# A transformer block's last additions: seven of eight moved beside the expert blocks, and cut in halves

## The chip, the cores and the metric

The kernel runs on one core of one Trainium2 chip. The metric is device microseconds of one execution. Before the change three runs took 1761.9, 1764.81 and 1767.08 us, median 1764.81 us. A separate execution was taken by the hardware profiler; all durations below come from that one.

## The reference, cut to what matters

`x` holds 8 batches of 512 tokens of 256 numbers, all float32. Four layers follow each other, each added to `x` after a layer norm: a decaying scan with projections, a mixture of experts, causal attention with 16 heads, and the same mixture of experts again.

```python
x = L0_attn_a_x                                  # (8, 512, 256)
x = x + scan(_layernorm(x), ...)
x = x + ffn(_layernorm(x), ...)                  # mixture 0
x = x + attention(_layernorm(x), ...)
x = x + ffn(_layernorm(x), ...)                  # mixture 1: the last thing computed
```

In a mixture a router picks 4 of 16 experts for every token (groups of four experts first, then the best in the two best groups), with weights that add up to 2.5. The output is the weighted sum of the four experts' outputs, plus that of shared experts that take every token:

```python
topk_idx, tw = _route(x, router_w, bias)
routed = sum over the 4 chosen e of tw[e] * ((silu(x @ gate_w[e]) * (x @ up_w[e])) @ down_w[e])
return routed + shared(x)
```

`setup_inputs(seed=0)` draws the inputs, so the number of tokens that each expert gets is fixed by the seed.

## The kernel before, in words

**Four stages.** Scan, mixture 0, attention, mixture 1. While a layer goes batch by batch, the router and the shared experts of the mixture behind it run beside it, and each token's row is scattered to DRAM (`xg`), into the regions of its four experts. When all batches are through, `routed(i, table, beside)` (L802) works off the experts' rows in blocks of 128.

**The blocks and their order.** Every expert's region is cut into blocks of 128 rows; within a region the tokens of batch 0 lie first, then those of batch 1, and so on. `blocks` writes the table of blocks: first the first block of every expert, then the second of every expert that has one, and so on. The program is built for `LIKELY` = 136 blocks (table entries behind the last real block do no harm); only if there are more does a branch run the other seven first.

**One block.** `load(n)` on SP's queue brings 128 rows from `xg` (L838). `fetch(n)` copies the expert's gate and up weights (ACT and DVE, L846). `turn(n)` transposes the rows on PE, `up(n)` does the gate and up products on PE (L864), sigmoid on ACT (L872) and two products on DVE (L873, L874), and the row's weight for this expert (L877, L885). `down(n)` does the last product (L892), ACT scales it by that weight (L900), and an indirect DMA on POOL's queue adds the 128 rows to the result in DRAM (L901). The result stands in two halves, `parts[1][0]` and `parts[1][1]`: even blocks add to the one, odd blocks to the other. The first also holds the layer's input, the second the shared experts' output. A scatter to a part waits until the one before it on the same part has landed.

**The loop.** `run` (L911) issues, for block n: the load of n + 2, the fetch of n + 1, `up(n)`, `turn(n + 1)`, `down(n - 2)`. Rows live in nine buffers (tag `kb4`), and a buffer is free again when the scatter of its block has landed. Behind `down(k - 1)` the loop calls what stands under key k in `beside`:

```python
if n - 2 >= first:
    down(n - 2)
    for work_beside in beside.get(n - 1, ()):
        work_beside()
```

**The last additions.** A batch's output is the sum of the two parts' rows of that batch. `sum_of(b, ...)` (L1387) loads both, 512 KB each, 4 KB for each of 128 partitions; `add_up` (L1398) adds them in one DVE instruction of 128 x 1024 (L1399) and stores 512 KB (L1402). `SUMMED` (L62) says for five batches after how many blocks this may be done beside the blocks, with all its DMAs on POOL's queue, where the scatters are too:

```python
SUMMED = {0: DONE[0], 1: 76, 2: 88, 3: 110, 4: 127}     # DONE[0] = 64
```

The loads go in at that key, the addition and the store eight blocks later. Batches 5, 6 and 7 are summed at the end (`at_the_end`, L1452), with part 0 loaded on SP's queue and part 1 on ACT's.

**The check.** Whether a batch is really complete after that many blocks depends on the routing. `check(b)` (L1420) works it out on DVE, at block 10 + 4b: `upto[b]` holds each expert's count after batch b; `most` is the largest of these counts in blocks, rounded up; `done` is the sum over all experts of min(the expert's blocks, `most`); the batch counts as late if `done > SUMMED[b]`. `checked` (block 40) adds up the late ones into `late`. Batch 0 is not checked, since after 64 blocks it is complete in any case. Behind the blocks SP, ACT and DVE load `late` (L1455) and branch (L1462): if it is above zero, all batches in `SUMMED` are summed once more at the end, and then those that are not in it:

```python
with tc.If(again > 0):
    for b in SUMMED:
        at_the_end(b)
for b in range(B):
    if b not in SUMMED:
        at_the_end(b)
```

**Order.** A scheduling layer sets the final order on each engine from the order written; what is marked `keep_in_program_order` stays where it is written. Every engine and every queue works in order. On POOL's queue a load of a sum waits for the last scatter to its part, and the next scatter to that part waits until the load has landed.

Of the kernel before, what the change touches and what calls it, by code (L numbers as in the profile page):

```python
# [10 lines left out]
FP = mybir.dt.float32  # L11
# [4 lines left out]
P = 128  # L16
B, T, D = 8, 512, 256
NT = T // P
# [22 lines left out]
LIKELY = TK * NTOK // BLK + E // 2  # L41
# [6 lines left out]
DONE = [min(E * (b + 1) * NT, NBLK) for b in range(B)]  # L48
# [6 lines left out]
KB, COLS = 9, 6  # L55
# [3 lines left out]
HELD = 6  # L59


SUMMED = {0: DONE[0], 1: 76, 2: 88, 3: 110, 4: 127}  # L62
PICKS = 5
ES, QK = 6, 6
ATT_SCALE = 0.25
# [9 lines left out]
def tile_hybrid_block(  # L75
# [22 lines left out]
    nc = tc.nc  # L98
# [3 lines left out]
    work = ctx.enter_context(tc.tile_pool(name="work", bufs=2))  # L102
# [8 lines left out]
    def banks_of(**many):  # L111
        pools = ExitStack()
        for kind, bufs in many.items():
            stage[kind] = pools.enter_context(
                tc.tile_pool(name=f"ps_{kind}", bufs=bufs, space=bass.MemoryType.PSUM)
            )
        return pools
# [7 lines left out]
    parts = [[dram.tile([NTOK + BLK, D], FP, name=f"part_{i}_{j}") for j in range(2)] for i in range(2)]  # L125
# [3 lines left out]
    def values(name: str):  # L129
        return work.tile([P, NT * (H * VC + 32 - VC)], FP, tag="v", name=name)  # L130
# [82 lines left out]
    def load_expert(e: int):  # L213
# [13 lines left out]
        out=before,  # L227
        in_=before,
# [20 lines left out]
    def load_attention_weights():  # L249
# [16 lines left out]
        out=causal, in_=causal, compare_op=ALU.is_ge, fill=0.0, base=0, pattern=[[0, 2], [1, P]], channel_multiplier=-1  # L266
# [6 lines left out]
        out=tri, in_=tri, compare_op=ALU.is_gt, fill=0.0, base=0, pattern=[[1, P]], channel_multiplier=-1  # L273
# [324 lines left out]
    def choices(i: int, b: int, tag: str, held, paced: bool):  # L598
# [59 lines left out]
        counts[i] = row[:, NT, :]  # L658
        if i == 1 and b in SUMMED:
            upto[b] = small.tile([1, E], FP, tag=f"upto_{b}", name=f"upto_{b}", bufs=1)  # L660
# [722 lines left out]
    with banks_of(big=4, misc=2, y=2):  # L1383

        beside = (nc.gpsimd, nc.gpsimd)

        def sum_of(b: int, homes, queues=(nc.sync, nc.scalar)):  # L1387

            both = []
            for j, queue in enumerate(queues):  # L1390
                both.append(homes(j))
                queue.dma_start(  # L1392
                    out=both[j],
                    in_=parts[1][j][b * T : (b + 1) * T, :].rearrange("(p t) d -> p (t d)", p=P),
                )
            return both

        def add_up(b: int, both, queues=(nc.sync, nc.scalar)):  # L1398
            added = nc.vector.tensor_add(both[0], both[0], both[1])  # L1399
            if queues is beside:  # L1400
                tc.keep_in_program_order(added)
            queues[b % 2].dma_start(out=out[b].rearrange("(p t) d -> p (t d)", p=P), in_=both[0])  # L1402

        sums = {}

        def early(b: int):
            def homes(j: int):
                tile = xpool.tile([P, NT, D], FP, tag="x", name=f"sum_{b}_0") if j == 0 else values(f"sum_{b}_1")
                return tile.rearrange("p t d -> p (t d)") if j == 0 else tile[:, 0 : NT * D]

            return {
                SUMMED[b]: [lambda: sums.update({b: sum_of(b, homes, beside)})],
                SUMMED[b] + 8: [lambda: add_up(b, sums.pop(b), beside)],
            }

        late = small.tile([1, 1], I32, tag="late", name="late", bufs=1)
        lates = small.tile([1, len(SUMMED)], FP, tag="lates", name="lates", bufs=1)
        nc.gpsimd.memset(lates, 0.0)

        def check(b: int):  # L1420


            nb = table[4]
            one = small.tile([1, E + 2], FP, tag="one", name=f"one_{b}", bufs=1)
            n, most, done = one[:, 0:E], one[:, E : E + 1], one[:, E + 1 : E + 2]
            nc.vector.tensor_sub(n, upto[b], region[0:1, :])
            shape = [1, E, NJ]
            more = work.tile(shape, FP, tag="col", name=f"above_{b}", bufs=COLS)
            nc.vector.tensor_tensor(
                more, n.unsqueeze(2).to_broadcast(shape), steps[0:1, :].unsqueeze(1).to_broadcast(shape), ALU.is_gt  # L1430
            )
            nc.vector.tensor_reduce(n, more, AX.X, ALU.add)
            nc.vector.tensor_reduce(most, n, AX.X, ALU.max)
            nc.vector.tensor_scalar(n, nb[0:1, :], most, None, ALU.min)
            nc.vector.tensor_reduce(done, n, AX.X, ALU.add)
            nc.vector.tensor_scalar(lates[:, b : b + 1], done, float(SUMMED[b]), None, ALU.is_gt)

        def checked():
            any_late = small.tile([1, 1], FP, tag="any_late", name="any_late", bufs=1)
            nc.vector.tensor_reduce(any_late, lates, AX.X, ALU.add)  # L1440
            nc.vector.tensor_copy(late, any_late)

        plan = {}
        for b in SUMMED:
            for at, do in early(b).items():
                plan.setdefault(at, []).extend(do)
            if SUMMED[b] < DONE[b]:
                plan.setdefault(10 + 4 * b, []).append(lambda b=b: check(b))
        plan.setdefault(40, []).append(checked)
        routed(1, table, plan)  # L1450

        def at_the_end(b: int):  # L1452
            add_up(b, sum_of(b, lambda j: work.tile([P, NT * D], FP, tag="kb4", name=f"sum_{b}_{j}", bufs=KB)))

        _, (again,) = nc.values_load_multi_w_load_instructions(  # L1455
            late,
            engines=[mybir.EngineType.SP, mybir.EngineType.Activation, mybir.EngineType.DVE],
            min_val=0,
            max_val=len(SUMMED),
            skip_runtime_bounds_check_because="a count of batches",  # L1460
# [7 lines that stand above are left out]
# [42 lines left out]
```

## Time and profile before

| what | us |
|---|---|
| median of three runs | 1764.81 |
| the profiled execution | 1766.56 |
| its span, first to last instruction | 1764.9 |
| PE busy over the span | 1678.5 (95%) |
| first and last scatter of mixture 1's blocks start | 1348.25, 1745.18 |
| last matmul of the blocks ends | about 1735.1 |
| first load of the last three sums starts | 1747.17 |
| last instruction of the chain, the third addition, starts | 1758.87 |

How to read it: in the list of groups a row is line, engine, operation, tile written and tile read, count, then busy time and mean nanoseconds of one, then the engine's idle time ahead of them and what ended it. A timeline row is start, length, engine, line, operation, tiles, count, and in brackets the idle time of that engine just before. In a table of windows the columns are the stretch, its length, busy time and count of PE, weight loads, DVE, ACT and POOL, then the granted TensorE clock, the mean share of the 16 DMA engines in use, and GB/s.

### The profile page before, as it was taken

How to read it: one execution, taken by the hardware profiler on the slowest of the kernel's cores; microseconds unless marked ns; L12 is line 12 of the kernel's file. 1: busy time of each engine (PE TensorE's matmuls, PEld its weight loads, DVE VectorE, ACT ScalarE, POOL GpSimd, SP SyncE). 2: the span in 40 equal slices, each digit the busy share in tenths (PEclk: the TensorE clock that was granted, in tenths of full speed). 3: DMA queues.
4: the chain of work that ended last, by engine and by line, in shares of the span. 5: the costliest groups of instructions: out<-in, count | busy, mean ns of one | idle time of the engine just before them, and what ended most of it. 6: DMA issues, size and time to landing. Idle time of an engine off the chain costs nothing. (4 is left out here: it accounts for less than half of the span.)

```text
span 1764.9 us, 32859 instructions
## 1 busy us (share of the span) xinstructions
PE 1678.5 (95%) x10640; PEld 1255.2 (71%) x10640; DVE 1097.8 (62%) x3429; ACT 806.3 (46%) x1739; POOL 773.4 (44%) x674
## 2 busy tenths in 40 slices
PE   6899998989999999999999999999998999999993
PEld 3566665579999999954545545544557999998992
DVE  8888777535555655566776666566643655555552
ACT  3223222145555555555655454464424555555551
POOL 3355555535554655530032232322542555555563
PEclk9999998999999999999999999999999999999996
DMA  5454423445555665531011212122543555566666
GB/s 157 143 181 145 135 102 106 157 82 94 98 94 104 104 102 94 100 71 37 25 57 55 75 51 68 48 77 79 175 148 76 96 97 95 109 126 136 121 126 163
DMA packets 149280, 181.38 MB, mean 103 GB/s; under 512 B 16145, under 2 KB 135985, under 8 KB 149105
## 3 DMA queue, kind: packets, MB, share of 16 engines
q0 software_dynamic: 54720, 82.57, 25.1%
q1 hardware_dynamic: 92576, 92.71, 17.7%
q10 hardware_dynamic: 1808, 3.93, 0.6%
q8 instruction: 89, 1.46, 0.3%
q14 instruction: 87, 0.70, 0.1%
HBM read 81.62 MB, written 97.53 MB: 102 GB/s over the span
## 5 line engine op out<-in xcount | busy, mean ns | idle before, releaser
L901 POOL DMA_INDIRECT part<-rows x272 | 427.2, 1570 | 346.8 <-ACT rows L900 254.3
L702 POOL DMA_INDIRECT xg<-sorted_m,slots_m x256 | 257.8, 1007 | 287.8 <-ACT slots_m L699 114.5
L864 PEld LDWEIGHTS ph<-rows,gate 128*128 128x128 f32 x2176 | 286.0, 192 | 16.1 <-ACT rows L854 1.5
L864 PE MATMUL ph<-rows,gate 128*128 128x128 f32 x2176 | 289.3, 276 | 0.6 <-ACT rows L854 0.6
L864 PE MATMUL ph<-rows,up 128*128 128x128 f32 x2176 | 289.1, 276 | 0.0
L892 PE MATMUL pyr<-w_all,rows 128*128 x1088 | 280.5, 380 | 0.5 <-DVE rstd_l L425 0.5
L864 PEld LDWEIGHTS ph<-rows,up 128*128 128x128 f32 x2176 | 266.5, 193 | 0.0
L872 ACT ACTIVATE rows<-ph 128x256 f32<-128x256 f32 x272 | 104.2, 383 | 329.8 <-PE ph L864 329.8
L873 DVE TENSOR_TENSOR rows<-ph,rows 128x256 f32<-128x256 f32 x272 | 115.1, 423 | 191.9 <-ACT rows L872 191.7
L892 PEld LDWEIGHTS pyr<-w_all,rows 128*128 128x128 f32 x1088 | 185.2, 191 | 14.7 <-ACT rows L900 0.8
L846 ACT COPY gate<-w_all 128x512 f32 x272 | 170.0, 626 | 14.3 <-PE ph L864 2.4
L1102 ACT ACTIVATE w_all<-ps_a 128x1024 f32<-128x1024 f32 x128 | 124.4, 1021 | 82.0 <-PE ps_a L1091 74.8
L846 DVE COPY up<-w_all 128x512 f32 x272 | 118.9, 438 | 34.7 <-PE ph L864 19.4
L900 ACT ACTIVATE rows<-pyr,gain 128x256 f32<-128x256 f32 x272 | 128.4, 472 | 14.9 <-PE pyr L892 13.3
L877 DVE SCALAR_TENSOR_TENSOR gain<-rows,expert_b 128x4 f32<-128x4 f32 x272 | 61.2, 225 | 109.1 <-ACT rows L900 80.4
L1091 PE MATMUL ps_a<-w_all 32*128 32x512 f32 (+3 forms) x1024 | 122.6, 474 | 6.8 <-ACT w_all L1102 5.4
L954 PE MATMUL pg_m<-xT_m,su_sb 128*128 128x512 f32 x256 | 127.3, 620 | 0.0
L954 PE MATMUL pg_m<-xT_m,sg_sb 128*128 128x512 f32 x256 | 123.4, 604 | 0.0
L874 DVE TENSOR_TENSOR rows<-ph,rows 128x256 f32<-128x256 f32 x272 | 115.1, 423 | 8.4
L982 PE MATMUL pd_m<-sd_sb,act_m 128*128 128x256 f32 x512 | 119.8, 382 | 0.0
L853 PE MATMUL pt<-ident,rows 128*128 128x128 f32 x544 | 105.2, 275 | 15.3 <-DMA rows<-xg 14.8
L982 PEld LDWEIGHTS pd_m<-sd_sb,act_m 128*128 128x128 f32 x512 | 95.5, 190 | 20.9 <-issue 4.7
(219 smaller groups left out, 2214.0 us busy)
## 6 DMA issues: line engine op xcount, KB each, us to landing
rows<-xg SPq DMA_DIRECT2D x272, 136.0 KB, 2.5
part<-x SPq DMA_DIRECT2D x16, 512.0 KB, 3.0
part<-ys_m SPq DMA_DIRECT2D x14, 512.0 KB, 3.1
w_all<-in_L_ffn_gate_w_dram SPq DMA_DIRECT2D x24, 256.0 KB, 4.9
w_all<-in_L_ffn_up_w_dram SPq DMA_DIRECT2D x24, 256.0 KB, 5.8
w_all<-in_L_ffn_down_w_dram SPq DMA_DIRECT2D x24, 256.0 KB, 5.8
sum<-part POOLq DMA_DIRECT2D x10, 512.0 KB, 4.1
xg<-zeros SPq DMA_DIRECT2D x34, 136.0 KB, 2.3
```

The source lines that it names most:

```text
L702: nc.gpsimd.indirect_dma_start(out=xg[i], out_offset=bass.IndirectOffsetOnAxis(ap=slots[:, at : at + 1], axis=0), in_=rows[:, t, :], in_of ...
L846: copy(here, w_all[:, bass.ds(held[n][0] + half * KD * F, KD * F)])
L864: nc.tensor.matmul(ph[:, s, f * P : (f + 1) * P], lhsT=both[s][:, k * F + f * P : k * F + (f + 1) * P], rhs=rows[:, ROW + k * P : ROW + (k ...
L873: nc.vector.tensor_mul(act, ph[:, 0, :], act)
L874: nc.vector.tensor_mul(act, ph[:, 1, :], act)
L892: nc.tensor.matmul(py, lhsT=act[:, f * P : (f + 1) * P], rhs=w_all[:, bass.ds(w + 2 * KD * F + f * D, D)], start=(f == 0), stop=(f == KF - 1),
L900: nc.scalar.mul(rows[:, 0:D], py, gain[:, TK : TK + 1])
L901: nc.gpsimd.indirect_dma_start(out=parts[i][n % 2], out_offset=bass.IndirectOffsetOnAxis(ap=rows[:, D + 2 * TK : D + 2 * TK + 1].bitcast(U ...
L954: nc.tensor.matmul(dst, lhsT=w[:, k, f * P : (f + 1) * P], rhs=xnT[:, k, :], start=(k == 0), stop=(k == KD - 1),)
L982: nc.tensor.matmul(py[:, j, :], lhsT=acts[n][:, f, t * P : (t + 1) * P], rhs=shared[n][3][:, f, :], start=(n == 0 and f == 0), stop=(n == ...
L1091: nc.tensor.matmul(ps[j // 2][:, j % 2, col : col + n], lhsT=k_sb[w][r, o, c * P : (c + 1) * P], rhs=q_sb[r, o, c * P : T], start=True, st ...
L1102: nc.scalar.activation(es[two], ps[two][:, :, 0:cols], AF.Exp, scale=ATT_SCALE)
```

## The change

`SUMMED` names seven batches, with keys about 15 blocks apart and earlier than before; batch 0's key of 40 is below 64, so it is checked too, and there are seven checks in place of four. The addition goes in two DVE instructions of 128 x 512 and two stores of 256 KB, at key + 6 and key + 8, on POOL's queue; for batch 6 (keys 135 and 136) the stores go on SP's queue. At the end only batch 7 is summed in any case. There, and in the branch for late batches, each sum's loads come in two pieces of 256 KB a part, the additions in halves, one half's store on SP's queue and the other's on ACT's, and the additions are held in program order.

```diff
-SUMMED = {0: DONE[0], 1: 76, 2: 88, 3: 110, 4: 127}
+SUMMED = {0: 40, 1: 54, 2: 68, 3: 84, 4: 100, 5: 115, 6: 129}
...
-        def sum_of(b: int, homes, queues=(nc.sync, nc.scalar)):
-
-            both = []
-            for j, queue in enumerate(queues):
-                both.append(homes(j))
-                queue.dma_start(
-                    out=both[j],
-                    in_=parts[1][j][b * T : (b + 1) * T, :].rearrange("(p t) d -> p (t d)", p=P),
-                )
+        def sum_of(b: int, homes, queues=(nc.sync, nc.scalar), pieces: int = 1):
+
+            both = [homes(j) for j in range(2)]
+            step = NT * D // pieces
+            for at in range(0, NT * D, step):
+                for j, queue in enumerate(queues):
+                    rows = parts[1][j][b * T : (b + 1) * T, :].rearrange("(p t) d -> p (t d)", p=P)
+                    queue.dma_start(out=both[j][:, at : at + step], in_=rows[:, at : at + step])
             return both
 
-        def add_up(b: int, both, queues=(nc.sync, nc.scalar)):
-            added = nc.vector.tensor_add(both[0], both[0], both[1])
-            if queues is beside:
-                tc.keep_in_program_order(added)
-            queues[b % 2].dma_start(out=out[b].rearrange("(p t) d -> p (t d)", p=P), in_=both[0])
+        def add_up(b: int, both, half: int, queue):
+
+            here = slice(half * NT // 2 * D, (half + 1) * NT // 2 * D)
+            added = nc.vector.tensor_add(both[0][:, here], both[0][:, here], both[1][:, here])
+            tc.keep_in_program_order(added)
+            queue.dma_start(out=out[b].rearrange("(p t) d -> p (t d)", p=P)[:, here], in_=both[0][:, here])
...
+            queue = nc.sync if SUMMED[b] + 8 > LIKELY else nc.gpsimd
             return {
                 SUMMED[b]: [lambda: sums.update({b: sum_of(b, homes, beside)})],
-                SUMMED[b] + 8: [lambda: add_up(b, sums.pop(b), beside)],
+                min(SUMMED[b] + 6, LIKELY - 1): [lambda: add_up(b, sums[b], 0, queue)],
+                min(SUMMED[b] + 8, LIKELY): [lambda: add_up(b, sums.pop(b), 1, queue)],
             }
...
         def at_the_end(b: int):
-            add_up(b, sum_of(b, lambda j: work.tile([P, NT * D], FP, tag="kb4", name=f"sum_{b}_{j}", bufs=KB)))
+            both = sum_of(
+                b, lambda j: work.tile([P, NT * D], FP, tag="kb4", name=f"sum_{b}_{j}", bufs=KB), pieces=2
+            )
+            for half, queue in enumerate((nc.sync, nc.scalar)):
+                add_up(b, both, half, queue)
```

## The prediction

> **What bounds the kernel now.** I read the page's groups first, then PE's busy time by stretches, then POOL's timeline, then the chain at the end.
>
> Stretches: while the blocks run PE has no slack, so only what stops PE or lies behind the last block counts. PE idles 3.4 us of 235 from 1500 on. Behind 1735 PE is done and 30 us of DMA follow.
>
> ```profile
> 1500.00:1735.00 235.00, 231.57 (x1762) 221.41 (x1760) 134.75 (x401) 126.41 (x318) 131.32 (x92) 1.00 0.64 121
> 1735.00:1747.00 12.00, 0.06 (x1) 0.00 (x0) 0.00 (x0) 0.47 (x1) 9.26 (x7) 0.61 0.59 98
> 1752.00:1756.00 4.00, 0.00 (x0) 0.00 (x0) 0.00 (x0) 0.00 (x0) 0.00 (x0) 0.50 1.01 410
> ```
>
> PE's idle time in the blocks is nearly all waits for a block's rows (2.79 of the 3.4 us here, soon after the sum at 88):
>
> ```profile
> 1618.51 0.41 PE L853 MATMUL pt<-ident,rows 128*128 128x128 f32 x2 [1.83 <-DMA rows<-xg]
> ...
> 1622.53 0.41 PE L853 MATMUL pt<-ident,rows 128*128 128x128 f32 x2 [0.96 <-DMA rows<-xg]
> ```
>
> POOL's timeline shows why. Scatters 0 to 62 start 2.87 us apart, PE's pace. A sum's loads then hold the queue: below, scatters 125 (1713.08) to 128 (1729.15) take 16.1 us for three blocks where the pace gives 8.6.
>
> ```profile
> 1713.08 1.55 POOL L901 DMA_INDIRECT part<-rows  x1 [0.30 <-ACT rows L854]
> 1717.02 0.59 POOL L1392 DMA_DIRECT2D sum<-part  x1 [2.39 <-DMA part<-rows]
> 1717.91 1.60 POOL L901 DMA_INDIRECT part<-rows  x1 [0.30 <-issue]
> 1721.72 1.55 POOL L901 DMA_INDIRECT part<-rows  x1 [2.21 <-ACT rows L854]
> 1723.36 0.59 POOL L1392 DMA_DIRECT2D sum<-part  x1
> 1729.15 2.22 POOL L901 DMA_INDIRECT part<-rows  x1 [5.20 <-ACT rows L900]
> ```
>
> The chain: the last scatter starts 9.9 us behind pace and lands at 1748.87; then three sums.
>
> ```profile
> 1745.18 3.69 DMA part<-rows
> ...
> 1750.06 8.69 DMA sum<-part
> ...
> 1758.87 1.22 DVE sum L1399
> ```
>
> From the first load (1747.17) to the end the three sums take 17.7 us.
>
> **First step: the check.** It decides which program runs. I counted the tokens that the reference's routing gives each expert in mixture 1, with its default seed. The largest count after batches 0 to 6 is 167, 331, 472, 622, 793, 953, 1101: 2, 3, 4, 5, 7, 8, 9 blocks. The experts have 8, 10, 6, 7, 7, 8, 8, 8, 10, 10, 9, 9, 7, 9, 9, 10 blocks (135). So `done` is 32, 48, 64, 80, 111, 123, 131. Against the old keys (none for batch 0, then 76, 88, 110, 127) none is late, and the trace agrees: only three sums at the end. Against 40, 54, 68, 84, 100, 115, 129 batches 4, 5 and 6 are late (111 > 100, 123 > 115, 131 > 129). One is enough: expert 8 needs a seventh block for batch 4, 793 against 768 rows. So the branch is taken and all seven batches are summed again, then batch 7: the tail has eight sums, not three, and the seven beside the blocks are paid for as well.
>
> **Second step: five more sums in the tail.** A sum moves 3 x 0.524 = 1.573 MB. Lower bound: the busiest stretch above, 410 GB/s, 3.84 us each. Upper bound: the old tail's own average with its start and end, 17.7 / 3 = 5.9 us. Two things speak for the middle. Half pieces have 2 KB a partition in place of 4 KB, and the page's queue q1 (packets near 1 KB) moved 92.71 MB in 17.7% of 1764.9 us, 297 GB/s, which would be 5.3 us. And SP's and ACT's queues carry loads and stores in one order, so a load stands behind a store that waits for an addition. The additions themselves (1.22 us a sum) stay below DMA. I take 4.9: 5 x 4.9 = +24.5, between +19.2 and +29.5. The last sum's halves let one half's store start ahead of the other's addition, half of 1.22 and a part of a store: -1, between 0 and -3.
>
> The Trainium skill ("DMA: Bandwidth & Descriptors", Where 436 GB/s comes from) holds that HBM, at about 358 GB/s a core, binds such transfers; the 410 GB/s row contradicts it. By the page a sum would take 4.4 us and five +22.0, an estimate from its figure.
>
> **Third step: sums beside the blocks, on POOL's queue.** Lateness jumps over three scatters by 6.1, 6.2, 5.7 us where the loads stand one scatter apart (62 to 65, 74 to 77, 86 to 89), 7.2 and 7.5 where two apart (108 to 111, 125 to 128). It falls again by 0.36, 0.26, 0.38, 0.43 us a block (65 to 74, 77 to 86, 89 to 108, 111 to 125), one store included; I take 0.37. Row buffers carry about 9 us: at 9.1 PE stopped 0.32 us, at 12.5 altogether 3.1 us. What exceeds 9 stops PE. In the new instruction order batches 1 and 5 have two scatters between their loads, the others one. Then:
> - 40: 6.1 late; 11 blocks later 2.0.
> - 54: +7.2 is 9.2, PE stops 0.2; then 4.9.
> - 68: 10.9, stops 1.9; after 13 blocks 4.2.
> - 84: 10.2, stops 1.2; 4.2. At 100 the same; after 12 blocks 4.6.
> - 115: 11.9, stops 2.9; 4.9.
> - 129: 10.9 late with no rows left to load; the end recovered 0.58 a block (128 to 135), so 5 blocks leave 8.0.
>
> Stops 7.4 plus 8.0 is 15.4, against 9.9 before: +5.5. A second store for each of six sums on POOL's queue: a store delayed its next scatter by up to 0.6 us (issue 1.18), or not at all where that scatter waited for a landing anyway: 0 to +3.6, I take +1.5. Sum +7. From below: the lateness repeats what before had, 0; from above, each of the two more sums costs a whole jump, 7.5 each: +15.
>
> **What I cost at nothing.** Three more checks on DVE at blocks 10, 30 and 34: about 2.5 us each (0.68 + 0.66 + 0.54 and three of 0.15, and a subtraction); PE was busy 10.00 of every 10 us from 1380 to 1420, where four of them ran, with DVE below 7.7 of 10. Without that cover: 7.5 us. The additions in halves stand at key + 6, two blocks earlier. In before the first sum's addition ran at 1546.39 and its second load, issued at 1535.79, had landed when scatter 65 started (1540.78); two blocks (5.7 us) earlier is 1540.7, just in time at 6 us of lateness. At 11 DVE waits 5 us with its later work behind it; PE needs a block's product about 4.5 us after DVE has made it (block 132: made by 1725.2, its last matmuls from 1729.65), so nearly all is covered, and it falls together with PE's stops for rows. Uncovered: up to 1 us in each of five sums.
>
> The Trainium skill ("Runtime: NRT & Kernel Launch", Instruction fetch mechanics) speaks against a taken branch: a target outside the fetched pages must be loaded first. Before, the branch on SP was followed 0.2 us later by its next instruction; a fetch here would hide while the queues wait for the last scatter.
>
> **Sum.** On the profiled execution: span 1764.9 + 24.5 - 1 + 7 = 1795.4 and 1.7 around it. That execution, 1766.56, was 1.75 above the median; on the median 1764.81 + 30.5 = 1795.3.
>
> **Rivals.**
> - Fallback taken, but POOL's queue costs no more than before: 1788 (1783 to 1792). For it: 14 to 16 blocks between sums, 12 before among the first three. Against: seven in a row, and the lateness left over at the next sum (2.9, then 6.8) grew.
> - Fallback taken and the stops multiply, DVE's early additions on top of the rows: 1807 to 1820. For it: the 5 us waits. Against: the 4.5 us of slack.
> - Other side: the branch is not taken, because the counts on the chip differ. The point is 768 rows for batch 4 and the like for 5 and 6. Then one sum is left: a load (4.1) with its add and store, about 9.5 in place of 17.7, -8.2. With +7 it gives 1763.6, without 1756.6.
>
> **How the numbers follow.** Three runs spread 0.3%, so 0.3% (5.3 us) is what tells from no change. Forecast 0.60 (1786 to 1807), no extra lateness 0.23, multiplied stops 0.12, branch not taken 0.05. The range 1782 to 1812 leaves out the last and half of the third. Only the last can be faster (0.03), same 0.01, or slower; the rest are slower.
>
> **What would show it.** After: 16 loads of 256 KB each on SP's and ACT's queues behind the last block, 30 half additions in all; the last scatter landing near 1756; PE's waits for rows in the blocks 6 to 9 us. Two loads on each queue would mean that the branch was not taken. A tail (first load to end) near 41 us is the forecast's; above 48, the pieces wait for each other more than I priced. The price of a sum in the tail is what I may most easily have wrong, then the lateness.

## The result, and the profile after

The changed kernel takes 1797.05 us (median of four runs, 1796.98 to 1800.92) against 1765.94 us before (median of four): a ratio of 1.0177, 95% interval 1.0158 to 1.0196, or 31.1 us more. Forecast was +30.5 us.

The profiled execution took 1796.98 us with a span of 1795.3 us, 30.4 us more than the span before. It divides at two events, the first and the last scatter of mixture 1's blocks:

| us | before | after | more |
|---|---|---|---|
| first scatter starts | 1348.25 | 1348.67 | 0.4 |
| first to last scatter (starts) | 396.9 | 402.7 | 5.75 |
| last scatter's start to the end of the span | 19.7 | 43.95 | 24.2 |

The last scatter lands at 1754.93 (before: 1748.87).

The operations on the tile `sum` in after (line, engine, operation, count, then shortest, median and longest in ns, first and last start) say which program ran:

```profile
L1400 DVE TENSOR_TENSOR sum<-sum,sum x30: 680/692/693, 1472.6 to 1790.8; 128x512 f32<-128x512 f32 x30
L1394 SPq DMA_DIRECT2D sum<-part x16: 319/323/689, 1753.4 to 1785.0; - x16
L1394 ACTq DMA_DIRECT2D sum<-part x16: 326/346/1185, 1755.0 to 1787.4; - x16
L1394 POOL DMA_DIRECT2D sum<-part x14: 586/596/1186, 1462.8 to 1735.1; - x14
```

Sixteen loads on each of SP's and ACT's queues, all behind 1753, are eight sums, each with two pieces of either part; 30 half additions are seven sums beside the blocks and eight at the end. So the branch was taken, and every early sum was made twice.

The chain of after, its end:

```profile
1735.10 0.90 DMA sum<-part
1735.99 14.64 DMA part<-rows x5
...
1751.35 3.58 DMA part<-rows
...
1755.01 5.43 DMA sum<-part
...
1784.42 2.43 DMA out_dram<-sum
...
1787.40 3.27 DMA sum<-part
...
1790.76 0.69 DVE sum L1400
```

Before, one piece of 8.69 us of `sum<-part` stood between the last scatter and the third addition; now five of 5.0 to 5.7 us, 26.5 us in all, stand between 1755.01 and 1784.42. Then comes something that before did not have: a store that lands (2.43 us) before the last sum's load may start (1787.40). The eighth sum's loads do not overlap the seventh's. Windows of after show it in the DMA engines (last two columns: mean share of the DMA engines, GB/s):

```profile
1500.00:1735.00 235.00, 227.82 (x1736) 217.82 (x1735) 132.08 (x403) 125.42 (x314) 134.45 (x99) 1.00 0.66 126
...
1774.00:1776.00 2.00, 0.00 (x0) 0.00 (x0) 1.32 (x2) 0.00 (x0) 0.00 (x0) 0.50 1.06 408
...
1784.00:1787.00 3.00, 0.00 (x0) 0.00 (x0) 0.39 (x1) 0.00 (x0) 0.00 (x0) 0.50 0.77 251
1787.00:1790.00 3.00, 0.00 (x0) 0.00 (x0) 0.06 (x1) 0.00 (x0) 0.00 (x0) 0.50 0.80 274
```

The first row is the blocks: PE idles 7.2 us of 235 where it idled 3.4. The waits of PE during the blocks, in after (waited-for operation, then total us, times, longest):

```profile
PE pt L853 <- DMA rows<-xg: 7.1, 8, 1.5
PE pyr L892 <- DVE rows L874: 2.7, 1, 2.7
```

The first line is the one that the forecast counted on, 7.1 us for rows. The second is new: one stop of 2.7 us, at 1741.22, for a product on DVE. DVE's timeline in after names what held it:

```profile
1698.70 0.69 DVE L1400 TENSOR_TENSOR sum<-sum,sum 128x512 f32<-128x512 f32 x1 [3.70 <-DMA sum<-part]
...
1738.98 1.29 DVE L1400 TENSOR_TENSOR sum<-sum,sum 128x512 f32<-128x512 f32 x2 [5.00 <-DMA sum<-part]
```

DVE stands 3.7 and 5.0 us in front of an addition whose loads have not landed. PE's stop follows the second of these, a wait for batch 6's loads. Six such waits add up to 21.7 us. Whether they cost time is a question for the runs.

### The profile page after: what moved, and what is told of

Read it like the earlier page. It is cut to its first block, busy times and chain, and to the rows that moved or that the text cites. A ratio compares the mean times of both kernels' runs of the same rounds, so it can differ in the third digit from the quotient of the medians.

```text
span 1795.3 us, 32999 instructions
## 1 busy us (share of the span) xinstructions
PE 1681.6 (94%) x10640; PEld 1256.0 (70%) x10640; DVE 1110.4 (62%) x3474; ACT 807.3 (45%) x1739; POOL 776.1 (43%) x685
## 5 line engine op out<-in xcount | busy, mean ns | idle before, releaser
L864 PEld LDWEIGHTS ph<-rows,gate 128*128 128x128 f32 x2176 | 286.1, 192 | 15.9 <-ACT rows L854 1.4
L892 PEld LDWEIGHTS pyr<-w_all,rows 128*128 128x128 f32 x1088 | 186.1, 191 | 18.3 <-issue 3.0
```

Source lines behind the costliest of these rows:

```text
L864: nc.tensor.matmul(ph[:, s, f * P : (f + 1) * P], lhsT=both[s][:, k * F + f * P : k * F + (f + 1) * P], rhs=rows[:, ROW + k * P : ROW + (k ...
L892: nc.tensor.matmul(py, lhsT=act[:, f * P : (f + 1) * P], rhs=w_all[:, bass.ds(w + 2 * KD * F + f * D, D)], start=(f == 0), stop=(f == KF - 1),
```

## The experiments

My theory: the loss is the taken branch (five more sums at the end), plus some 6 us of lateness of POOL's queue. Rivals: the sums beside the blocks cost the time by themselves; halves, or DVE's early additions, cost it. For every run the table splits the profiled span at the same events as above, which takes out what happens in the stages ahead. The runs were made on several chips, two of them about 1% slower than the others (the kernel before took 1767.31, 1783.8, 1784.0 and 1769.59 us beside the four groups), so across groups the ratios are compared. Each ratio is against the kernel before on the same chip. On the two slower chips the blocks start 14 to 24 us later (1364.0 to 1370.5 us, on the others 1346.9 to 1350.4), which is about the whole difference, so it lies ahead of the stages in the table. Each of these stages is read from one profiled execution.

| kernel | first to last scatter | last scatter to end | ratio, 95% interval |
|---|---|---|---|
| before | 396.9 | 19.7 | 1 |
| after | 402.7 | 43.95 | 1.0177 [1.0158, 1.0196] |
| branch off | 401.4 | 12.7 | 1.0001 [0.9984, 1.0017] |
| all eight sums at the end, no branch | 385.7 | 41.35 | 1.0058 [1.0041, 1.0075] |
| before, branch taken | 398.1 | 42.2 | 1.0134 [1.0112, 1.0156] |
| after, old places | 397.0 | 20.95 | 1.0029 [1.0017, 1.0042] |
| places that the routing allows | 409.2 | 13.0 | 1.0003 [0.9984, 1.0023] |
| the same, no waits between sums and scatters | 387.0 | 16.3 | 0.9927 [0.9899, 0.9955] |
| the same, one of the two waits left | 393.0 | 12.6 | 0.9941 [0.9920, 0.9961] |
| after, later additions | 406.3 | 48.3 | 1.0188 [1.0148, 1.0227] |
| no waits, three sums at the end | 385.9 | 20.3 | 0.9957 [0.9942, 0.9973] |
| no waits, seven beside, again | 386.6 | 16.8 | 0.9940 [0.9922, 0.9958] |
| the same, last stores on POOL | 386.6 | 16.2 | 0.9921 [0.9891, 0.9952] |

At PE's pace of 2.867 us the 135 steps from the first to the last scatter take 387.0 us; what stands above that in the second column is lateness.

### The branch off

```diff
-            nc.vector.tensor_scalar(lates[:, b : b + 1], done, float(SUMMED[b]), None, ALU.is_gt)
+            nc.vector.tensor_scalar(lates[:, b : b + 1], done, float(SUMMED[b] + NBLK), None, ALU.is_gt)
```

> The changed kernel with the check's threshold raised by 143 blocks, so that no batch counts as late and only batch 7 is summed at the end; batches 4, 5 and 6 keep the sums made beside the blocks, which lack the blocks still to come. My theory (the branch is taken and its seven sums are most of the loss): the last scatter lands near 1755 as in the changed kernel, the tail falls from 41.9 us to 9 to 11, so about 1766 us (1763 to 1769), within 5 us of before. Rival (the sums beside the blocks cost most of the loss): it stays above 1780. Rival (the branch was not the cause of the eight sums): nothing moves, 1797.

Measured: 1765.99 us, ratio 1.0001 [0.9984, 1.0017]. The whole loss of 1.77% is gone, with sums, halves, stores and lateness beside the blocks left in. SP's timeline has two loads behind the blocks:

```profile
1750.74 0.80 SPq L1394 DMA_DIRECT2D sum<-part  x2
1756.87 0.34 SPq L1402 DMA_DIRECT2D out_dram<-sum  x1
```

They start 2.1 us after the last scatter (1748.63); in after SP's first load started 2.0 us after it (1753.38 against 1751.35). So entering the branch adds nothing to the time. SP executes its branch instruction in after at 1741.3, 12 us ahead of its first load, and that load waits for the second to last scatter in any case; what the entry costs is hidden there. The same run answers what the change would be worth if no batch were late: the tail is 7 us shorter, the blocks 4.5 us longer, and the medians show no difference.

### The branch in the kernel before

```diff
-            nc.vector.tensor_scalar(lates[:, b : b + 1], done, float(SUMMED[b]), None, ALU.is_gt)
+            nc.vector.tensor_scalar(lates[:, b : b + 1], done, float(SUMMED[b] - NBLK), None, ALU.is_gt)
```

> The kernel before with the check's threshold lowered by 143 blocks, so that its checked batches count as late: five whole sums beside the blocks as before, then the branch sums all five again and three more follow, in whole pieces of 512 KB. My theory (each further sum in the tail costs 4.4 to 5.3 us, whatever the piece): the last scatter lands at 1749 as before, the tail grows from 17.7 us to 40 to 45: 1788 to 1794 us. If whole pieces move much better than halves, the tail is 36 us or less (under 1785); if the branch has a price of its own above the sums, over 1796.

Measured: 1791.38 us, ratio 1.0134 [1.0112, 1.0156], as expected. The old kernel with its branch forced pays 24.1 us of the 31.1, and its tail grows by 22.5 us. That is 4.5 us for each of the five sums, exit of the branch included. After pays a longer tail by 1.8 us and 4.6 us more between the scatters.

### All eight sums at the end, without a branch

```diff
-        routed(1, table, plan)
+        routed(1, table, {})
...
-        with tc.If(again > 0):
-            for b in SUMMED:
-                at_the_end(b)
         for b in range(B):
-            if b not in SUMMED:
-                at_the_end(b)
+            at_the_end(b)
```

> No sum beside the blocks, no check and no branch: all eight batches are summed at the end in halves. My theory (sums on POOL's queue make the last scatter 15 us late against PE's pace and PE's stops are a part of that): PE waits for rows under 0.5 us in the blocks, the last scatter lands at 1739 to 1743, and the tail of eight sums takes 37 to 41 us, since the seventh and eighth now overlap: 1778 to 1785 us. If the branch itself (its code, the way out of it) is a large part of the tail, the tail is 32 us or less and the time under 1775. If lateness on POOL's queue costs nothing, the last scatter lands near 1755 still and the time is above 1792.

Measured: 1776.82 us, ratio 1.0058 [1.0041, 1.0075], a little below what I expected. PE never waits for rows in this run, and the last scatter has no lateness at all (385.7 us), as expected. The tail of eight is 41.35 us, 2.6 us shorter than the same eight behind a branch. Its queues show why. ACT's timeline at the end of this kernel:

```profile
1765.88 0.33 ACTq L1394 DMA_DIRECT2D sum<-part  x1
1767.91 4.21 ACTq L1402 DMA_DIRECT2D out_dram<-sum  x2
```

and of after:

```profile
1780.56 4.21 ACTq L1402 DMA_DIRECT2D out_dram<-sum  x2
1787.03 0.83 ACTq L1394 DMA_DIRECT2D sum<-part  x2
```

Without the branch the eighth sum's last load stands ahead of the seventh's stores. In after both of ACT's loads for it stand behind these stores, since the branch must be left first, and wait 2.4 us more for a store to land. The exit is a wall in the order of the program, not a costly instruction: SP's next load starts 0.4 us after its branch instruction (1784.60, 1784.2). Counted from the last scatter, the seventh sum's last store goes out after 33.1 us in after (1784.42) and after 34.1 us without the branch (1767.91); from there to the end it takes 10.9 and 7.3 us.

Against the kernel before, with five sums beside the blocks, making none there costs 0.58%, and making seven, with the branch off, gains nothing.

### Halves alone

```diff
-SUMMED = {0: 40, 1: 54, 2: 68, 3: 84, 4: 100, 5: 115, 6: 129}
+SUMMED = {0: DONE[0], 1: 76, 2: 88, 3: 110, 4: 127}
```

> The keys of before (64, 76, 88, 110, 127), the halves of the change: additions in halves at key + 6 and key + 8, two stores each, the last three sums in two pieces a part. My theory: second stores on POOL's queue cost 0 to 3 us, the last three sums in halves gain 0 to 3 us, DVE's early additions under 1 us a sum: 1762 to 1769 us, the same as before within noise. Rival (halves are what costs): above 1772.

Measured: 1771.68 us, ratio 1.0029 [1.0017, 1.0042]: 4.4 us slower where I expected no change or a small gain. The scatters take 397.0 us (396.9 before), so the second store of each sum on POOL's queue costs nothing. The tail of three is 1.25 us longer, not 0 to 3 us shorter. The other 3 us lie ahead of the first scatter (1350.11 against 1348.25) or outside the profiled execution. The old code with its branch forced also started at 1350.41, and the branch-off kernel at 1347.21, so that start moves without cause in these lines. I do not claim more than the 1.25 us for the halves.

Where the 1.25 us come from can be read in SP's and ACT's queues. Before, all six loads go out in one stretch:

```profile
1747.17 1.35 SPq L1392 DMA_DIRECT2D sum<-part  x3
1749.01 2.05 ACTq L1392 DMA_DIRECT2D sum<-part  x3
```

With halves there are twelve, and both queues stop on the way:

```profile
1748.84 3.74 SPq L1394 DMA_DIRECT2D sum<-part  x5
1757.02 0.34 SPq L1402 DMA_DIRECT2D out_dram<-sum  x1
1757.42 0.42 SPq L1394 DMA_DIRECT2D sum<-part  x1
1751.69 6.55 ACTq L1394 DMA_DIRECT2D sum<-part  x6
```

SP's last load stands behind a store that waits for an addition. ACT's last load goes out at 1757.91, just when a load that started at 1752.09 has landed; before, ACT's last load went out at 1750.06. So the last load lands 16.5 us after the last scatter, where it landed after 13.6. From there to the end it is shorter with halves, 4.4 us against 6.15. No run changed the order of issue alone, so this account is read from the traces and not tested.

### Places that the routing allows

```diff
-SUMMED = {0: 40, 1: 54, 2: 68, 3: 84, 4: 100, 5: 115, 6: 129}
+SUMMED = {0: 40, 1: 54, 2: 68, 3: 84, 4: 112, 5: 124, 6: 132}
```

> The change with keys that fit the routing: 112, 124 and 132 for batches 4, 5 and 6 (done is 111, 123, 131), all else as changed. My theory (the branch was most of the loss, the lateness on POOL's queue eats what the two sums fewer in the tail give): no batch is late, one sum at the end, its tail 9 us from the last landing as with the branch off; but three sums 8 to 12 blocks apart leave the last scatter 16 to 20 us behind pace, more than the 14.2 with the branch off: 1764 to 1772 us, between the same as before and 0.4% slower. Rival (with the branch gone the two sums fewer show as a gain): under 1760.

Measured: ratio 1.0003 [0.9984, 1.0023]. The three late places are mended, the branch is not taken, the tail is 13.0 us, and still nothing is gained: the scatters take 409.2 us, 22 us above PE's pace, somewhat more than the 16 to 20 that I expected, in an execution that lay 6 us above the run's median. Three sums now stand within the last 26 blocks: the lateness is 8.8 us at scatter 108, ahead of them, and 22 at the last. What the tail gives, POOL's queue takes.

### The two waits between sums and scatters

On POOL's queue a sum's load waits for the last scatter to its part, and the next scatter waits for that load, though they touch rows of different batches. In the next kernel the loads stand two blocks later and in program order, behind two more scatters, and neither waits for the other.

```diff
+            if i == 1:
+                tc.declare_no_dep(scatter.ins, group="sums", reason="rows of later batches")
+                tc.add_to_no_dep_group("scatters", scatter.ins)
...
+                    if queues is beside:
+                        tc.keep_in_program_order(made)
+                        tc.declare_no_dep(made.ins, group="scatters", reason="scatters two back have landed")
+                        tc.add_to_no_dep_group("sums", made.ins)
...
-                SUMMED[b]: [lambda: sums.update({b: sum_of(b, homes, beside)})],
+                SUMMED[b] + 2: [lambda: sums.update({b: sum_of(b, homes, beside)})],
```

> The keys of the run with right keys, and the loads of the sums two blocks later on POOL's queue, with no waits between them and the scatters: the rows of a finished batch are written by no later scatter, and the scatters that wrote them have landed, because each scatter waits for the one before it on its part. My theory (the two waits, the load's for the last scatter and the next scatter's for the load, are the whole lateness): jumps of 6 to 7.5 us per sum fall under 2, PE's waits for rows under 1 us in the blocks, the last scatter lands at 1737 to 1743 and one sum follows in 9 to 10: 1748 to 1756 us, faster than both. Rival (DMA's load from the sums is what delays the scatters): lateness stays above 6 us and the time above 1760.

Measured: ratio 0.9927 [0.9899, 0.9955], 11.9 us faster than the kernel before. That is within what I expected, with a longer tail than I had thought (16.3 us from the last scatter's start). The scatters take 387.0 us: no lateness left at the end. On the way it reaches 4.2 us behind a sum, and PE never waits for rows. POOL's timeline in after, around batch 6's loads:

```profile
1729.85 0.60 POOL L1394 DMA_DIRECT2D sum<-part  x1 [2.56 <-DMA part<-rows]
1730.75 1.60 POOL L901 DMA_INDIRECT part<-rows  x1 [0.30 <-ACT rows L900]
1735.10 0.59 POOL L1394 DMA_DIRECT2D sum<-part  x1 [2.75 <-DMA part<-rows]
1735.99 1.59 POOL L901 DMA_INDIRECT part<-rows  x1 [0.30 <-issue]
1740.35 1.54 POOL L901 DMA_INDIRECT part<-rows  x1 [2.77 <-DMA part<-rows]
```

and in the kernel without the waits, around batch 5's:

```profile
1723.96 1.55 POOL L901 DMA_INDIRECT part<-rows  x1 [1.33 <-ACT rows L900]
1724.94 1.77 POOL L1397 DMA_DIRECT2D sum<-part  x2
1727.01 1.64 POOL L901 DMA_INDIRECT part<-rows  x1 [0.30 <-issue]
1729.92 1.58 POOL L901 DMA_INDIRECT part<-rows  x1 [1.27 <-ACT rows L900]
```

In the upper view each load is issued after 2.6 to 2.8 us of waiting for a scatter to land, and the scatter after the second one waits again. In the lower both loads go out in one stretch of 1.77 us, and the scatters around them keep steps of about 3 us.

To see which of the two waits matters, the load's own wait was put back, with the loads at the same places as in the run with the places that the routing allows. The edit, beside the places:

```diff
+            if i == 1:
+                tc.declare_no_dep(scatter.ins, group="sums", reason="rows of later batches")
...
+                    if queues is beside:
+                        tc.add_to_no_dep_group("sums", made.ins)
```

> As the run without false waits, but with the load's wait for the scatter before it left in, at the same keys as the run with right keys; only the next scatter's wait for the load is taken away. My theory: the load still holds POOL's queue until a scatter has landed, 2.5 us or so for each of a sum's two loads, so a jump is 3 to 5 us in place of 6 to 7.5, and with recovery of 0.35 a block the lateness at the end is 6 to 11: 1756 to 1764 us. If the next scatter's wait is all that counts: 1748 to 1756. If it counts for nothing: as with right keys.

Measured: ratio 0.9941 [0.9920, 0.9961]. The time lies on the border between my range and that of the rival for which the scatter's wait is all that counts. The scatters take 393.0 us, a lateness of 6 us, the low end of what I expected. So of the 22 us of lateness with both waits, the scatter's wait for the load accounts for about 16, and the load's wait together with its place two blocks earlier for the last 6; no run separates these two. The split is rough: the profiled execution with both waits lay 6 us above its own median. By the medians on this chip, taking the scatter's wait away gives 12.1 us (1785.42 to 1773.37), and the rest 1.5 us more (1771.88), which is not told apart from nothing, as the 6 us are set against a tail that is 3.7 us shorter here.

### Later additions

```diff
-                min(SUMMED[b] + 6, LIKELY - 1): [lambda: add_up(b, sums[b], 0, queue)],
-                min(SUMMED[b] + 8, LIKELY): [lambda: add_up(b, sums.pop(b), 1, queue)],
+                min(SUMMED[b] + 10, LIKELY - 1): [lambda: add_up(b, sums[b], 0, queue)],
+                min(SUMMED[b] + 12, LIKELY): [lambda: add_up(b, sums.pop(b), 1, queue)],
```

> The change with its additions at key + 10 and key + 12 in place of + 6 and + 8 (batch 6's stay at the last two blocks), branch taken as before. My theory (DVE's waits of 3 to 4 us for a sum's loads are covered): those waits of batches 1, 3, 4 and 5 vanish, PE's waits for rows stay at 6 to 9 us, 1794 to 1799 us. Rival (DVE's early additions cost PE time): 1791 or less.

Measured: ratio 1.0188 [1.0148, 1.0227] against 1.0177 [1.0158, 1.0196] for after, which ran on another chip; the two are not told apart. DVE's waits in this run hold one line for sums:

```profile
DVE sum L1400 <- DMA sum<-part: 6.2, 1, 6.2
```

PE's waits in the blocks of the same run:

```profile
PE pt L853 <- DMA rows<-xg: 8.3, 7, 2.4
PE pyr L892 <- DVE rows L874: 3.9, 1, 3.9
```

Five of DVE's six waits are gone (21.7 us down to 6.2, batch 6's alone), and nothing is faster: PE waits 8.3 us for rows instead of 7.1. Batch 6's additions were not moved, and behind them stands PE's one stop for a product again, 3.9 us. The chain of after does pass through the wait at 1698.70, yet without it nothing was gained. The kernel without the waits between sums and scatters says the same: there DVE waits 17.5 us for sums' loads, in six waits, and neither PE nor the last scatter is late. The tail of this run is 48.3 us against 43.95 in after, though the code behind the blocks is the same. That is one execution on another chip, and the cause is open.

### How much of the gain is the waits, how much the sums

```diff
-SUMMED = {0: 40, 1: 54, 2: 68, 3: 84, 4: 112, 5: 124, 6: 132}
+SUMMED = {0: DONE[0], 1: 76, 2: 88, 3: 110, 4: 127}
```

(against the kernel without the waits)

> This is the version with both false waits taken away, but with the old places of the sums: five beside the blocks (at 62, 76, 88, 110, 127), three behind them. It tells how much of the gain of that version comes from taking the waits away and how much from having two sums fewer at the end. If the waits alone were what the old plan lost, scatter 135 keeps within 1 us of its pace where it was 9.9 late, the three sums at the end take 16 to 19 us from the landing as before, and the whole comes out 8 to 10 us under the kernel before, -0.45% to -0.6%. With the two sums fewer at the end worth some 8 us on top, the version with seven sums beside should then lie 8 us below this one, near -1.0%; as it measured -0.73%, I expect rather that each part gives about half: -0.25% to -0.5% here. Rival: without the waits the scatters and loads share DMA so that the sums at the end give nothing, and both versions measure alike, -0.7%.

> The version with seven sums at the blocks that the routing allows and both false waits taken away, once more on the chip that runs the version with three sums at the end, so that the two are compared under one kernel before. Expected -0.6% to -0.9% against the kernel before, 4 to 8 us below the version with three sums at the end.

Measured: 0.9957 [0.9942, 0.9973] with three sums at the end, 0.9940 [0.9922, 0.9958] with one. Against the kernel before, taking the waits away from the old plan gives 0.43%, within what I expected. But this kernel also has the halves, which made the old plan 0.29% slower: against that kernel (1.0029, on another chip) the gain is about 0.7%, and the two stages together fall by 11.8 us. The places are not quite the old ones either. In the trace batch 4's two loads do not stand behind scatter 128: all four loads of batches 3 and 4 go out between 1690.1 and 1695.0, around scatter 112, so the mark to keep them in program order did not hold them there. Two sums fewer at the end add 4.1 us by the medians, at the low end of what I expected, and the two intervals overlap. The stages agree with a small gain of the two sums: 385.9 and 386.6 us between the scatters, 20.3 and 16.8 us behind. The tail falls by 3.5 us for two sums, though one costs 4.1 us (20.4 / 5 from the runs above); the next run looks for what holds the last sum.

### What holds the last sum

```diff
-            queue = nc.sync if SUMMED[b] + 8 > LIKELY else nc.gpsimd
+            queue = nc.gpsimd
...
+            if SUMMED[b] + 8 > LIKELY:
+                return {
+                    SUMMED[b] + 2: [lambda: sums.update({b: sum_of(b, homes, beside)})],
+                    LIKELY: [lambda: add_up(b, sums[b], 0, queue), lambda: add_up(b, sums.pop(b), 1, queue)],
+                }
```

> The version with seven sums beside the blocks and both waits taken away, with one thing moved: batch 6's two stores stand on POOL's queue behind the last scatter, where they stood on SP's queue ahead of the last sum's loads (and both of its additions behind the last block). In that version SP issued those stores at 1755.88 and the last sum's first load only at 1759.21, though the last scatter started at 1752.23; from that scatter to the end it took 16.3 us, against 12.7 in the kernel with the branch off, where SP's queue was free (loads at 1750.74, last scatter 1748.63). If SP's queue is what holds the last sum, its first load goes out within 3 us of the last scatter and the tail from there is 12.5 to 14 us: 2.5 to 3.5 us less, -0.75% to -0.9% against the kernel before. Rival: batch 6's own loads fill the DMA engines until then, so the last sum's loads only share with them, and the tail stays at 16 us and the ratio at -0.6% to -0.75%.

Measured: 1752.18 us against 1769.59, ratio 0.9921 [0.9891, 0.9952], the lowest here, though not told apart from the version it came from. The ratio lies in the range of my theory and its interval covers the rival's too, but the tail of 16.2 us is the rival's: my theory of SP's queue fell. SP's and ACT's first loads are no longer behind a store and start 4.9 us after the last scatter (1733.48), 2 us sooner than in the version that it came from, yet the tail is as long as there. The chain's end in this kernel:

```profile
1728.52 3.69 DMA part<-rows
1733.48 4.80 DMA part<-rows
1738.91 6.57 DMA sum<-part
```

The last scatter lands in 4.8 us (3.58 in after) and the last sum's load takes 6.57 us, against 4.83 in the version that it came from. That fits sharing with batch 6's loads and stores. The table agrees: where batch 6's loads stand two blocks earlier or more, one sum's tail is 12.6 to 13.0 us (three kernels), where they stand right ahead of the last two scatters 16.2 to 16.8 (three kernels). No run moved those loads alone, so the sharing is argued, not shown.

## Why the prediction was right

**The check.** Right, and it decided the case. The counts of the routing said 4, 5 and 6 late; the trace has 16 loads on each queue, and with the branch off the loss is gone (1.0001).

**Five more sums in the tail.** The term was +24.5 (and -1 for halves); the tail grew by 24.2. The total was right and its parts were not, so that it came so close is luck. Step by step, from one profiled execution of each kernel: halves on three sums +1.25 (old places), five more sums without a branch 41.35 - 20.95 = 20.4 or 4.1 each, the exit of the branch +2.6. So the 4.9 was above the mark for a sum and had no term for the wall behind the branch. The gain that I saw in "one half's store start ahead of the other's addition" is there: from the landing of the last load to the end it takes 4.6 us in after and took 6.15 before. But the halves also delay the last loads, for which I had no term, and that is more. Of the two reasons that I gave for the middle of the range, the rate of 297 GB/s was too low: after moved 360 GB/s in the mean from 1755 to 1784, and 408 in its busiest 2 us. Stores in the way of loads is right, most of all at the exit.

On the rate, the Trainium skill ("DMA: Bandwidth & Descriptors", Where 436 GB/s comes from) has HBM bind at about 358 GB/s a core. 408 GB/s here is above it again, and without the branch every window of 2 us from 1752 to 1770 is, with 373 to 408 GB/s; so it was no ceiling here. The mean over the whole stretch of loads and stores is another matter: 360 GB/s in after and 358 without the branch (1738 to 1768), with the DMA engines in use 1.00 and 0.99 of the time. Five sums at 4.1 us each are 386 GB/s. The page's estimate of +22.0 lies nearer to the measured 20.4 than my 24.5 does: with the DMA engines in use all the time the price of one more sum fits a rate, and what I put on top of it was too much.

**Sums beside the blocks.** "Stops 7.4 plus 8.0" was +5.5 against before; PE's waits for rows are 7.1 us and the scatters take 5.75 us longer. The hand count of 15.4 us of lateness met 15.6, and it held on the way too: with the stops included it has 11.1, 12.3, 13.5, 16.4 and 18.3 us behind the sums at 68, 84, 100, 115 and 129, and the scatters of after stand up to 12.0, 14.8, 15.9, 18.1 and 19.0 us behind PE's pace there. PE's stops are 9.8 us in place of 7.4, as the one of 2.7 us for DVE's product was not in it, and what is left of the lateness is 5.8 in place of 8.0. "A second store for each of six sums ... I take +1.5" was wrong: 0.1 us (old places). The sum of +7 stands against 5.75, plus 0.4 us of a later start.

**What was costed at nothing.** The three more checks cost nothing: up to scatter 37, behind all of them, the scatters of after keep within 0.5 us of PE's pace. The additions two blocks early were bounded as 5 us of DVE's waiting, and just that appeared. For five of the sums the cover held: in the run with later additions their waits are gone and nothing is faster. For batch 6 it did not: PE stopped 2.7 us where the step allowed up to 1 us for a sum. No run shows whether that stop cost time; POOL's queue was 18 to 19 us behind at that point.

**Instruction fetch.** The Trainium skill ("Runtime: NRT & Kernel Launch", Instruction fetch mechanics) has a taken branch wait for its target to be loaded where that lies outside the fetched pages. If it did, it was hidden, as forecast: 2.0 us from last scatter to first load with the branch taken, 2.1 without. No run here shows such a load by itself.

**The rivals.** A branch not taken was put at 1763.6 against 1764.81 before, a ratio of 0.999; the run with the branch off measured 1.0001. The rival whose stops multiply falls with the 7.1 us of waits for rows, where the forecast has 7.4. The rival without extra lateness falls with the 5.75 us more from the first to the last scatter.

## What to carry to other kernels

Where work is moved earlier on the word of a check at run time, work out from the data what the check will answer before pricing anything else: here it turned 7 us less in the tail into 24 us more. Where a queue works in order, ask what each transfer put between others waits for, and what waits for it: two waits between rows that never overlap cost up to 22 us of lateness, more than the moved sums could give back, and taking them away was worth 0.4% on the old plan, 0.7% against the old plan with halves. A branch that is taken costs less by its entry than by what can no longer overlap across its end.

## What the runs showed of the hardware

- Entering the branch added nothing to the time, though the code of seven sums lies inside: SP's branch instruction (1741.3) stood 12 us ahead of the scatter's landing that its first load waited for. Where it is not hidden it shows, even when the branch is not taken: in the kernel without the waits SP's branch instruction stands at 1757.5, behind batch 6's stores, and the first load at 1759.21, 1.7 us later; how much of that is the branch is not known. Leaving the taken branch cost 2.6 us, by the tails of two executions (43.95 and 41.35); the same end took 48.3 in the run with later additions, so the figure is rough.
- 256 KB pieces in place of 512 KB made the tail of three sums 1.25 us longer. The end is shorter by 1.7 us (4.4 against 6.15), but counted from the last scatter the last loads go out 7.3 us later on SP's queue and 5.9 us on ACT's, as both queues stop between the pieces.
- Two loads and a scatter that do not wait for each other run side by side at little cost to the scatters: these fall 3.5 to 4.3 us behind PE's pace for a while and catch up, with 385.9 to 387.0 us from first to last in four kernels, at most 1.3 us more than with no sums there at all (385.7).
- The time at which the blocks start moved between 1347.2 and 1350.4 us on one chip among kernels that are alike up to there. Differences of 2 to 3 us in the whole span are better read by stages.
